# A recurrent block with six layers of local attention: the decays of a state in a PSUM bank, two small products more, and another order of the steps

## The chip, the cores and the metric

The kernel runs on one core of a Trainium2 chip. The time is the device time of one execution in microseconds. The kernel before took 3447.9 us, the median of three runs (3443.46 to 3448.29).

## The reference

The input x has 16 sequences of 256 rows of 128 numbers. After a layer norm two branches are computed from it, and their product is added to x.

```python
x = L0_attn_x
xn = _layernorm(x, axis=-1)
s = _L0_attn_ref(xn, ...)              # selective scan, 16 states per channel
g = _silu(_L0_ffn_ref(xn, ...))        # six layers of local attention and feed-forward
x = x + s * g
```

The first branch is a selective scan. With delta, u, B and C computed from xn by projections and short convolutions, each channel has 16 states, and state n decays with A = -(n + 1):

```python
dA = jnp.exp(d_t[..., None] * A)
h = dA * h + (d_t * u_t)[..., None] * B_t[:, None, :]
y = jnp.einsum('bdn,bn->bd', h, C_t)
```

The second branch has six layers. Each has 16 heads of width 64 with normed and rotated q and k, a softmax over a window of 32 rows and the 32 before them, an output product, and a gated feed-forward (gelu, inner width 341).

## The kernel before, in words

All work is laid out in iterations. A block is 128 rows of one sequence; a layer has 32 blocks and the six layers have 192. Iteration n does one step of each of many stages, for blocks at different distances: block n + 4 is projected to q and k, squared and rotated, block n + 2 is scaled and transposed, block n + 1 is scored, and block n is attended, divided and transposed. The list `order` (L759) says in which order the stages of one iteration are issued. The kernel is written with a manual schedule, so every engine takes its instructions in just that order, and waits at each until what it needs is there.

The attention runs so: `project` multiplies the rows with the q and k weights (L427), `values` with those of v. `square` (ACT, L438) and `lengths` (DVE, L504) make the sums of squares, `guess` (DVE) and `refine` (POOL) the inverse roots of two blocks at once, `rotate`, `rotate2` (DVE, L448 and L459) and `add` (POOL, L470) turn q and k, and `scale` (POOL, L542) multiplies with the inverse lengths. `turn` transposes q and k on PE (L552), and `turned_q` and `turned_k` copy them out of PSUM on ACT (L556). `score` writes a mask and then the products (L587, L601), `greatest` and `subtract` (DVE, L614 and L624) and `soften` (ACT, L633) make the weights, `turn_weights` and `turned_weights` transpose them, `attend` multiplies with the values (L657), and `divide_last` and `divide` (L673 to L681) divide. The last pair of heads (c = 7) has banks of its own, "e" and "l". `turn_out` and `turned_out` transpose the result, and after the second block of a sequence `close` multiplies with the output weights (L708): its first half ends an odd block's iteration, its second half belongs to the next iteration, as does `residual` (L718). `hand_out` copies v out of PSUM (L480) and lays it out with eight or ten DMAs on SP (L491 to L494).

The feed-forward of four blocks (a group of two sequences) is a generator of twelve pieces. `feed` takes the next piece and stands three times in `order`, so a group's feed-forward lasts four iterations: transposes and row statistics in the third piece, the norm in the fourth, transposes in the sixth, the first products in the ninth (L349, with gelu at L357), and the second in the eleventh (L372, with its residual at L375). In the last layer `end` (L388) follows when the last piece of a group is done: silu, the product with the first branch, four transposes on PE (L401), an add and a store.

The selective scan goes along with it: eight groups of 512 columns, one state per iteration. `clock` gives n from -2 to 17 for each group. `bring` loads the rows of B and C of state n + 2 to all partitions (SP), `decay` takes the exponential for the decays of state n + 1 (ACT, L296), `drive` multiplies B of state n + 1 with du (POOL, L301), `advance` scans state n (DVE, L288), `weigh` multiplies state n - 1 with C and adds it to y (POOL, L281 and L282), and `put_out` makes the output product. `before_scan`, taken a piece at a time by `prepare`, computes the next group's delta, du, B and C, with two convolutions on DVE (L220 and L227).

PSUM is one tile of eight banks of 512 numbers. The table `where` (L44) gives each use its bank; a name used by `pair` takes that bank and the next. A step that writes a bank waits until the earlier readers of that bank are done, so `where` and `order` together set the waits.

## Time and profile before

| | |
|---|---|
| runs | 3447.9 us median, 3443.46 to 3448.29 |
| the profiled execution | 3446.38 us, of which its span is 3444.6 us |
| PE busy | 3238.9 us (94%) |
| DVE busy | 2810.2 us (82%) |
| POOL busy | 2598.0 us (75%) |
| ACT busy | 2123.3 us (62%) |
| mean granted PE clock | 0.988 |
| scan, L288 | 128 times, 277.3 us, 2.17 us each |
| decays, L296 | 128 times, 80.6 us, 0.63 us each |

Busy time is the time in which an engine works at an instruction. PE is the matrix engine, PEld its loading of weights, DVE the vector engine, ACT the scalar engine, POOL the general one, and SP the one that issues most DMAs. In a group line the name before the arrow is what is written and the names behind it are what is read, with the number of instructions behind an x. What stands behind a vertical bar or in square brackets is idle time of the engine just before, and what ended it. In a line of a timeline the first number is the start and the second the length.

### The profile page before, as it was taken

Reading aid. Unit: us, or ns where it says so; the run is one execution under the profiler, and the core shown is the slowest. Engines: PE = TensorE matmul, PEld = TensorE weight load, DVE = VectorE, ACT = ScalarE, POOL = GpSimd, SP = SyncE. Lnnn points to the kernel's source line nnn. Section 1 sums busy time; section 2 is a strip of 40 time slices with the busy share of each in tenths; the row PEclk is TensorE's granted clock in tenths of the full one; section 3 lists DMA queues with packets and bytes.
Section 4 is the critical chain, followed back from the end, with each engine's and each line's share of the span. In section 5 each row is a group of like instructions: output and inputs, shape, how many; then the busy total and the mean of one; then the engine's idle time right before and its main releaser. Section 6 shows DMA issues by size and latency. Waiting matters only on the chain.

```text
span 3444.6 us, 139812 instructions
## 1 busy us (share of the span) xinstructions
PE 3238.9 (94%) x62080; PEld 2163.4 (63%) x62080; DVE 2810.2 (82%) x3705; ACT 2123.3 (62%) x2725; POOL 2598.0 (75%) x2358
## 2 busy tenths in 40 slices
PE   6999999999999999999999999999999999999986
PEld 3666666666666666666666666666666666666663
DVE  6898879887898789878987889788879987777663
ACT  4666657655666566656665666576666665666554
POOL 6688868986898589968996789688878996565550
PEclk9999999999999999999999999999999999999998
DMA  3433334433333334333333333334333432222222
GB/s 87 104 98 105 84 84 104 104 81 83 97 97 90 91 94 97 91 85 88 107 92 91 88 96 92 89 99 98 91 81 93 105 94 70 69 64 70 63 64 57
DMA packets 190680, 304.49 MB, mean 88 GB/s; under 512 B 32702, under 2 KB 56572, under 8 KB 190076
## 3 DMA queue, kind: packets, MB, share of 16 engines
q1 hardware_dynamic: 189788, 295.22, 33.9%
q8 instruction: 488, 8.00, 1.0%
q14 instruction: 116, 0.95, 0.1%
q10 hardware_dynamic: 288, 0.33, 0.0%
HBM read 94.81 MB, written 8.91 MB: 30 GB/s over the span
## 4 chain that ended last, share of the span: by engine, by line
PE 73%; DVE 12%; ACT 6%; POOL 5%; issue 4%; DMA 0%; SPq 0%; DVEq 0%; ACTq 0%; POOLq 0%
PE psum L427 23%; PE psum L552 14%; PE psum L708 9%; PE psum L657 7%; PE psum L349 7%; PE psum L601 6%; PE psum L372 3%; ACT oT L556 3%; DVE t L459 2%; DVE o L681 2%; PE psum L587 2%; DVE hs L288 1%; DVE t L448 1%; POOL t L470 1%; DVE cv L227 1%
## 5 line engine op out<-in xcount | busy, mean ns | idle before, releaser
L470 POOL TENSOR_TENSOR t<-t,t 128x1024 f32<-128x1024 f32 x384 | 957.1, 2502 | 355.0 <-DVE t L459 184.4
L427 PE MATMUL psum<-wqkv,xT 128*128 128x512 f32 x2304 | 1070.3, 600 | 18.6 <-DVE cv L227 7.2
L542 POOL TENSOR_TENSOR t<-t,y 128x1024 f32<-128x1024 f32 x384 | 723.1, 1905 | 7.5
L427 PEld LDWEIGHTS psum<-wqkv,xT 128*128 128x128 f32 x2304 | 417.4, 192 | 406.0 <-issue 304.5
L448 DVE TENSOR_TENSOR t<-psum,tab 128x1024 f32<-128x1024 f32 x384 | 467.9, 1219 | 143.9 <-PE psum L427 131.1
L556 ACT COPY aT<-psum 128x1024 f32<-128x1024 f32 x192 | 194.2, 1012 | 589.6 <-PE psum L552 589.6
L459 DVE TENSOR_TENSOR t<-psum,tab 128x1024 f32<-128x1024 f32 x384 | 465.9, 1213 | 0.0
L504 DVE TENSOR_REDUCE ss<-sq 128x16 f32<-128x1024 f32 x384 | 456.4, 1198 | 1.3
L552 PE MATMUL psum<-ident,t 128*128 128x128 f32 x3072 | 412.7, 277 | 20.8 <-POOL t L542 8.9
L438 ACT ACTIVATE sq<-psum 128x1024 f32<-128x1024 f32 x384 | 395.0, 1029 | 51.4 <-DVE t L459 51.0
L657 PEld LDWEIGHTS psum<-v,aT 64*32 64x32 f32 x24576 | 294.0, 105 | 200.9 <-issue 121.9
L708 PE MATMUL psum<-oT,wo 128*128 128x256 f32 x1536 | 357.5, 386 | 24.2 <-ACT oT L556 24.2
L657 PE MATMUL psum<-v,aT 64*32 64x65 f32 x24576 | 332.8, 227 | 47.0 <-issue 24.6
L552 PEld LDWEIGHTS psum<-ident,t 128*128 128x128 f32 x3072 | 340.4, 142 | 40.3 <-POOL t L542 11.7
L708 PEld LDWEIGHTS psum<-oT,wo 128*128 128x128 f32 x1536 | 283.8, 190 | 81.4 <-ACT oT L556 46.5
L480 ACT COPY vt<-psum 128x1024 f32<-128x1024 f32 x192 | 196.2, 1022 | 189.6 <-PE psum L427 189.6
L601 PEld LDWEIGHTS psum<-kT,qT 64*32 64x32 f32 x24576 | 282.8, 105 | 11.2 <-issue 0.8
L601 PE MATMUL psum<-kT,qT 64*32 64x64 f32 x24576 | 286.2, 226 | 0.0
L288 DVE TENSOR_TENSOR_SCAN hs<-dA,bc 128x512 f32<-128x512 f32 x128 | 277.3, 2166 | 0.0
L556 ACT COPY oT<-psum 128x1024 f32<-128x1024 f32 x192 | 194.8, 1014 | 124.9 <-PE psum L552 123.0
L349 PE MATMUL psum<-xn,w 128*128 128x512 f32 (+1 forms) x576 | 260.2, 601 | 6.0 <-ACT o L674 4.8
L624 DVE TENSOR_TENSOR at<-psum,top 128x1024 f32<-128x1024 f32 x192 | 235.1, 1225 | 25.3
(102 smaller groups left out, 4583.0 us busy)
## 6 DMA issues: line engine op xcount, KB each, us to landing
v<-vt SPq DMA_DIRECT2D x1152, 130.0 KB, 2.4
bc<-rows SPq DMA_DIRECT2D x128, 512.0 KB, 5.1
v<-vt SPq DMA_DIRECT2D x576, 65.0 KB, 2.5
wqkv<-in_Wqkv SPq DMA_DIRECT2D x18, 512.0 KB, 4.0
wo<-in_Wo SPq DMA_DIRECT2D x6, 512.0 KB, 4.0
first<-in_x SPq DMA_DIRECT2D x8, 256.0 KB, 5.0
xn<-xT SPq DMA_DIRECT2D x16, 128.0 KB, 2.4
pad<-xn SPq DMA_DIRECT2D x8, 256.0 KB
```

The costliest lines, as they stand in the source:

```text
L349: nc.tensor.matmul(ph[0:n, i * G : (i + 1) * G], w1[:, i * DI + c0 : i * DI + c0 + n], xn, start=True, stop=True,)
L427: nc.tensor.matmul(pq[:, cc], xb, wq[:, cc], start=True, stop=True)
L448: nc.vector.tensor_tensor(t1.rearrange("p (h d) -> p h d", h=H), b["pq", i].rearrange("p (h d) -> p h d", h=H), table(n, i, 0).unsqueeze(1 ...
L459: nc.vector.tensor_tensor(t2.rearrange("p (h f d) -> p h f d", h=H, f=2), b["pq", i].rearrange("p (h f d) -> p h f d", h=H, f=2)[:, :, ::- ...
L470: nc.gpsimd.tensor_tensor(b["qk", i], b["qk", i], b["t2", i], ALU.add)
L504: nc.vector.tensor_reduce(b["ss"][:, j * H : (j + 1) * H], b["sq", i].rearrange("p (h d) -> p h d", h=H), AX.X, ALU.add,)
L542: nc.gpsimd.tensor_tensor(t3, t3, b["inv"][:, j * H : (j + 1) * H].unsqueeze(2).to_broadcast([128, H, DH]), ALU.mult,)
L552: nc.tensor.transpose(pt[:, cc], of[:, cc], ident)
L556: nc.scalar.copy(to, pt.rearrange("p (c t) -> p c t", c=NP))
L601: nc.tensor.matmul(sc4[jj, r, c, :], qT[rr, c, jj], kT[rr, c, k0 : k0 + 64], start=False, stop=True, skip_group_check=True,)
L657: nc.tensor.matmul(b["pav7"][r][jj, 0:VW] if c == 7 else b["pav"][jj, r, c, :], aT[rr, c, jj], v2[rr, j, c * VW : (c + 1) * VW], start=Tru ...
L708: nc.tensor.matmul(b["pw"][:, 0:L], wo[:, c, :], b["oT"][:, c, :], start=(c == 0), stop=(c == NP - 1), skip_group_check=True,)
```

## The change

There are three parts. The decays of state n are written into PSUM bank 0 (name "d") in the same iteration in which they are scanned, in place of an SBUF tile one iteration ahead; bank 0 is also the first bank of k. In `attend`, two products of four columns come before the others, one for each half of the rows, into the banks of the last pair of heads, where the products of c = 7 then write over them. And `where` and `order` are others. In the new order the scan stands after the residual near the start of an iteration, v is projected right behind q, k is projected behind the transposes of the weights, k's transposes follow q's, and `soften` stands before two of the three `feed`.

```diff
-    where = dict(q="6", k="0", v="4", qT="4", kT="0", s="2", w="4", av="2", o="2", h0="6", h1="0", h2="4", e="7", l="6", pw="4", f="7", n="1")
+    where = dict(q="6", k="0", v="4", qT="2", kT="6", s="2", w="4", av="4", o="4", h0="2", h1="0", h2="4", e="3", l="2", pw="1", f="2", n="3", d="0")
...
     def decay():
         g, n = now
-        if 0 <= n + 1 < NS:
-            dA[n + 1] = mb.tile([128, G], FP, name="dA", bufs=2)
-            nc.scalar.activation(dA[n + 1], of[g]["delta"], AF.Exp, scale=-float(n + 2))
+        if 0 <= n < NS:
+            dA[n] = bank("d")
+            nc.scalar.activation(dA[n], of[g]["delta"], AF.Exp, scale=-float(n + 1))
...
         b["pav7"] = [bank("e"), bank("l")]
+
+        for r in range(2):
+            rr = slice(r * 64, (r + 1) * 64)
+            nc.tensor.matmul(
+                b["pav7"][r][0:W, 0:4], aT[rr, 7, 0:W], v2[rr, :, 0], start=True, stop=True
+            )
         for c in (7, 0, 1, 2, 3, 4, 5, 6):
```

The order of one iteration after the change, whole (that of before is at L759 to L807):

```python
    order = (
        (state, None, decay),
        (lengths, 3, 1),
        (norms_on, None),
        (guess, 3),
        (close, -1, 1),
        (residual, -1),
        (prepare, None),
        (project, 4, 0),
        (state, None, advance),
        (values, 1),
        (hand_out, 1),
        (feed, None),
        (score, 1),
        (refine, 3),
        (scale, 2, 0),
        (rotate, 4, 0),
        (greatest, 1),
        (turn_weights, 0),
        (project, 4, 1),
        (scale, 2, 1),
        (turned_weights, 0),
        (subtract, 1),
        (attend, 0),
        (state, None, weigh),
        (square, 4, 0),
        (divide_last, 0),
        (turn, 2, 0),
        (rotate2, 4, 0),
        (square, 4, 1),
        (turn, 2, 1),
        (turned_q, 2),
        (divide, 0),
        (turned_k, 2),
        (add, 4, 0),
        (rotate, 4, 1),
        (turn_out, 0),
        (rotate2, 4, 1),
        (lengths, 4, 0),
        (turned_out, 0),
        (state, None, bring),
        (soften, 1),
        (state, None, put_out),
        (feed, None),
        (state, None, drive),
        (add, 4, 1),
        (feed, None),
        (close, 0, 0),
    )
```

More of the change, by code (lines that the diff above doesn't have):

```diff
@@ L759, in tile_kernel @@
     order = (
+        (state, None, decay),
+        (lengths, 3, 1),
         (norms_on, None),
-        (lengths, 3, 1),
         (guess, 3),
@@ L764, in tile_kernel @@
         (residual, -1),
+        (prepare, None),
+        (project, 4, 0),
+        (state, None, advance),
+        (values, 1),
+        (hand_out, 1),
         (feed, None),
-        (project, 4, 0),
-        (prepare, None),
         (score, 1),
+        (refine, 3),
+        (scale, 2, 0),
         (rotate, 4, 0),
+        (greatest, 1),
         (turn_weights, 0),
-        (rotate2, 4, 0),
-        (greatest, 1),
-        (state, None, weigh),
-        (refine, 3),
-        (subtract, 1),
-        (scale, 2, 0),
-        (turned_weights, 0),
-        (project, 4, 1),
-        (square, 4, 0),
-        (state, None, bring),
-        (values, 1),
-        (scale, 2, 1),
+        (project, 4, 1),
+        (scale, 2, 1),
+        (turned_weights, 0),
+        (subtract, 1),
+        (attend, 0),
+        (state, None, weigh),
+        (square, 4, 0),
+        (divide_last, 0),
+        (turn, 2, 0),
+        (rotate2, 4, 0),
+        (square, 4, 1),
+        (turn, 2, 1),
+        (turned_q, 2),
+        (divide, 0),
+        (turned_k, 2),
         (add, 4, 0),
         (rotate, 4, 1),
-        (state, None, decay),
-        (hand_out, 1),
+        (turn_out, 0),
         (rotate2, 4, 1),
-        (add, 4, 1),
-        (attend, 0),
-        (divide_last, 0),
-        (state, None, drive),
-        (turn, 2, 0),
-        (divide, 0),
-        (state, None, advance),
-        (square, 4, 1),
-        (lengths, 4, 0),
-        (turned_q, 2),
-        (feed, None),
-        (feed, None),
-        (state, None, put_out),
-        (turn_out, 0),
-        (turned_out, 0),
-        (turn, 2, 1),
-        (turned_k, 2),
+        (lengths, 4, 0),
+        (turned_out, 0),
+        (state, None, bring),
+        (soften, 1),
+        (state, None, put_out),
+        (feed, None),
+        (state, None, drive),
+        (add, 4, 1),
+        (feed, None),
         (close, 0, 0),
-        (soften, 1),
     )
```

## The prediction

> **What bounds the kernel now.** I read the page's busy shares first, then the chain that ended last, then the queues in order of time.

> ```profile
> span 3444.6 us, 139812 instructions
> PE 3238.9 (94%) x62080; PEld 2163.4 (63%) x62080; DVE 2810.2 (82%) x3705; ACT 2123.3 (62%) x2725; POOL 2598.0 (75%) x2358
> PE 73%; DVE 12%; ACT 6%; POOL 5%; issue 4%; DMA 0%; SPq 0%; DVEq 0%; ACTq 0%; POOLq 0%
> ```

> TensorE (PE) sets the pace and nearly fills the span. So a gain on another engine counts only where PE waits for it. The busy times by stretch show how little that is in a stage that repeats (four iterations, 66.8 us) and in the last layer:

> ```profile
> 2600.00:2666.80 66.80, 65.72 (x1292) 44.36 (x1291) 60.84 (x77) 42.68 (x55) 60.94 (x53) 1.00 0.37 94
> 3000.00:3074.50 74.50, 68.22 (x1294) 45.75 (x1293) 51.90 (x73) 43.81 (x56) 40.89 (x41) 0.95 0.26 67
> ```

> The columns are the stretch, then PE, weight loads, DVE, ACT and POOL busy, the granted clock, and DMA. PE is busy 65.7 of 66.8 us, but the last layer takes 74.5 us for less work on DVE and POOL. The PE timeline gives the price of each step (start, length):

> ```profile
> 2601.40 0.41 PE L587 MATMUL psum<-mask,ident_h 64*32 64x512 bf16 x8
> 2603.07 1.09 PE L552 MATMUL psum<-ident,at 128*128 128x128 f32 x8
> 2604.00 3.60 PE L427 MATMUL psum<-wqkv,xT 128*128 128x512 f32 x8
> 2607.53 1.74 PE L657 MATMUL psum<-v,aT 64*32 64x65 f32 x128
> 2609.20 1.09 PE L552 MATMUL psum<-ident,t 128*128 128x128 f32 x8
> 2623.76 5.42 PE L349 MATMUL psum<-xn,w 128*128 128x512 f32 x12 [0.46 <-ACT o L674]
> 2631.16 3.72 PE L708 MATMUL psum<-oT,wo 128*128 128x256 f32 x16 [0.23 <-ACT oT L556]
> ```

> From start to next start: score 1.7, eight transposes 0.9, a projection 1.8, attend 1.7, half of close 1.7, first feed-forward products 5.2 (the second ones, at L372, 2.6). An iteration without feed-forward is then three projections 5.4, score 1.7, four transpose groups 3.5, attend 1.7, half a close 1.7: 14.0. Four of them with one feed-forward (5.2 + 2.6 + two transpose groups 0.9) come to 64.8, so some 2 of the 66.8 us are waits, in six or so places.

> **The change part by part.**

> *The scan.* Now a scan at L288 takes from 1.21 to 3.37 us (median 2.09), because it and POOL take turns:

> ```profile
> 2610.39 5.62 POOL L470 TENSOR_TENSOR t<-t,t 128x1024 f32<-128x1024 f32 x2
> 2610.68 3.16 DVE L288 TENSOR_TENSOR_SCAN hs<-dA,bc 128x512 f32<-128x512 f32 x1
> 2613.76 2.31 DVE L504 TENSOR_REDUCE ss<-sq 128x16 f32<-128x1024 f32 x2
> ```

> The scan starts inside POOL's first add (2.37 alone), ends 1.1 us after that one, and the second add takes 3.3. [...] DVE saves 277.3 − 128 × 1.21 = 122 us; POOL loses the long forms of L470 and L301, about 100 us. Neither is on PE's path: worth nothing by itself, and a margin below. The write at L296 is 0.63 us of ACT before; into PSUM I take the same. Its bank 0 is k's: the second projection now waits for the scan.

> *The order.* I follow one iteration through the queues, from PE's first q projection at 0, in iterations that end with a close ("odd"); the others ("even") begin with its second half, 1.7 us, and everything follows 1.7 later. PE: q and v to 3.6, score to 5.3, transposed weights and k to 8.0. Behind the last score the maximum starts 0.18 after the transposes do, subtract starts 1.35 later and takes 1.23: 8.05. Since e and l are now banks 3 and 2, the whole attend waits for that subtract: 8.1, where before it stood behind both k and v and only its later products touched those banks. Attend and the small products to 10.0, turned q to 10.85, turned k to 11.7, turned out to 12.6 (divide: 0.33 after attend, 0.28, 1.09, in time). ACT's copy of oT comes 1.1 after the start of its transposes and takes 1.0: 13.85; rotate2 of k, behind divide on DVE, ends at 13.8. Both hold back close (its bank 1 is k's), so PE waits 0.9 to 1.3 us where it waited 0.5. Close to 15.6.

> Even: the same chain puts attend at 9.8 and the end of turned out at 14.3; kT is copied behind qT on ACT until 14.7, and the next q, in banks 6 and 7, starts at 14.75.

> Feed-forward pieces fill these holes. Four iterations are: odd with small transposes 15.6; even with small transposes 14.75; odd with the 5.2 before close, where PE does not wait any more, 12.6 + 5.2 + 1.7 = 19.5; even with the 2.6 at the end 14.3 + 2.6 = 16.9. Together 66.8, against 66.8: the waits change place and the sum does not move. Taken as 0 ± 30 us over the 47 groups.

> Covers: k's wait for the scan is hidden in even iterations (residual ends at 3.0, scan at 4.2, k starts at 7.9). In odd ones DVE comes 1.7 us late with the lengths, starts the scan at 3.0 and ends the first rotate at 5.3, 0.2 before the maximum can start; what makes it later than that goes into attend one for one. decay stands behind soften on ACT and ends at 3.0 in the worst case, just in time. drive is issued on POOL late in the iteration before and ends 1.4 into this one. POOL, from the guess: refine 3.9, scales 3.8, weigh 2.6, add, drive 1.3, add, done 1.5 us before its next refine. On SP, hand_out's DMAs go out from 6.4 on, one iteration before attend reads them; bring now stands behind them and behind weigh (about 12.3), lands 5.1 us later, and drive reads it more than 10 us after that. Convolution (3.1 us of DVE, bank 3) now holds back score instead of k: about 2 us a group in odd iterations, where the waits for L227 now sum to 24 us over eight groups. first_norm uses the same bank, behind evictions long done.

> *The small products* do not exist in before. They are two of L657's kind on two of its eight tiles, each twice like every fp32 product here. Lower bound: two shares of 128 in 1.7 us, 0.03 us. Upper bound: they run alone (weights 0.105 and matmul 0.23 of those rows, twice) 0.4 us with the queue's extra waits (0.05 each) for the DMAs that they gather. I take 0.2, nearest to two sets of eight at the row's rate (0.1 each); 192 × 0.2 = 38 us, in the 66.8 above.

> *The last layer.* Each group ends with silu, product and transposes (L395 to L401), and PE has nothing else queued:

> ```profile
> 3059.37 1.53 DVE L375 SCALAR_TENSOR_TENSOR xT<-psum,b,xT 64x512 f32<-64x512 f32 x2 [1.08 <-PE psum L372]
> 3061.99 1.07 ACT L633 ACTIVATE at<-at 128x1024 f32<-128x1024 f32 x1
> 3063.07 1.28 ACT L395 ACT_TABLE_LOAD   x1
> 3064.37 1.28 ACT L395 ACTIVATE xn<-xT 64x512 f32<-64x512 f32 x2
> 3065.68 0.69 DVE L397 TENSOR_TENSOR xn<-xn,sT 128x512 f32<-128x512 f32 x1 [4.78 <-ACT xn L395]
> 3066.43 1.11 PE L401 MATMUL psum<-ident,xn 128*128 128x128 f32 x4 [5.42 <-DVE xn L397]
> ```

> xT is ready at 3060.9, but silu waits behind oT, kT, soften and a table load. In after, soften and the load come before xT is ready; the transposes of o and k (1.7 us), which stand behind L372 now, move ahead of it. From L372's end: 0.3, 1.5, last half of silu 0.6, product 0.7, in all some 3.4 us of idle PE instead of 5.4: 2.0 saved. [...] Six gaps × (2.0 + 1.4) = 20 us; with no change of clock 12.

> *Scattered waits.* The waits name DVE and POOL in some 100 places (us in total, times, longest):

> ```profile
> PEld psum L552 <- DVE o L681: 29.5, 76, 1.5
> PEld psum L657 <- DVE at L624: 17.9, 20, 1.2
> PEld psum L552 <- POOL t L542: 11.7, 13, 2.5
> ```

> About 60 us; part of it lies behind long scans and goes with them, part comes back in other places: 15, between 0 and 45.

> **Sum.** The profiled execution took 3446.4 us (its span and 1.8 around it; the median of the runs is 1.5 above): 3446 − 20 − 15 ± 0 = 3411.

> **Rivals.** (1) *Slower: DVE's 0.2 us in odd iterations is gone.* If the scan still takes 2.17 or waits for drive, attend comes 0.75 later in two of four iterations, in the 32 groups with scans: 48 us, so 3459; it outweighs the gains from a delay of 0.55 on (a scan of about 1.75 or more). [...] (2) *Same:* the small products cost 0.4, 38 more: 3449. The two-tile form runs alone, which speaks for it; that they overlap with what stands in the queue, against. (3) *Faster still:* small products at 0.05 and feed-forward pieces hiding most of close's wait, 0.8 and 0.3 per group less: 3411 − 29 − 14 = 3368. (4) *The scan is not faster and nobody cares:* only the last layer gains, 3426.

> **How the numbers follow.** Chances: my forecast 40%, (4) 8%, (3) 12%, (2) 10%, (1) and its like 30%. Measurements of this kernel tell no change from 0.2%, 7 us (the three runs lie within 5). Faster 40 + 8 + 12, less 3 for the forecast's own tail: 57%; same 11%; slower 32%. The likeliest case's own range is 3380 to 3440; for 8 in 10 I reach to (3) and past (1): 3365 to 3478.

> **What would show it.** L288 at 1.21 to 1.3 throughout and no L470 above 2.4: the scan step. Attend's first load released by L624, close by oT at about 1 us: the order. L655's two rows and the distance to the first L663: 0.2. Gaps of 3.4 before L401. I am wrong if maximum waits for DVE rather than for score, or if POOL's drive releases the scan.

## Result: slower by 3.4%, where 1.1% faster was forecast

The changed kernel takes 3561.4 us (median of 4 runs, 3556.8 to 3574.8), the kernel before 3448.1 us beside it. The ratio is 1.034, with a 95% interval of 1.032 to 1.036. Forecast were 3411 us and a range of 3365 to 3478: the sign was wrong, and the range did not hold the time.

The page of the changed kernel (span, busy shares, chain that ended last):

```profile
span 3555.0 us, 141696 instructions
PE 3290.0 (93%) x62848; PEld 2227.4 (63%) x62848; DVE 2699.4 (76%) x3705; ACT 2107.5 (59%) x2725; POOL 2488.4 (70%) x2358
PE 82%; ACT 5%; issue 5%; DVE 3%; DMA 3%; POOL 1%; SPq 0%; ACTq 0%; POOLq 0%; DVEq 0%
```

DVE and POOL lost about 110 us each, as forecast; PE is busy 51 us longer, and the span grew by 110. The groups of instructions show that the scan did what was expected of it, and what the small products (L655) are busy:

```profile
L470 POOL TENSOR_TENSOR t<-t,t 128x1024 f32<-128x1024 f32 x384 | 908.1, 2365 | 525.4 <-DVE t L459 264.0 <-PE psum L663 223.6 <-DVE den L686 29.2
L288 DVE TENSOR_TENSOR_SCAN hs<-psum,bc 128x512 f32<-128x512 f32 x128 | 156.5, 1223 | 21.1 <-issue 13.2 <-POOL less L170 3.9
L655 PE MATMUL psum<-v,aT 64*32 64x4 f32 x768 | 74.8, 168 | 26.2 <-ACT sq L438 7.8 <-ACT aT L556 6.2 <-issue 2.7
```

The waits of PE, with the us in total, how many, and the longest:

```profile
PE psum L663 <- issue: 64.6, 29, 5.2
PE psum L714 <- ACT oT L556: 38.6, 48, 1.3
PE psum L401 <- DVE xn L397: 36.1, 8, 5.4
PE psum L552 <- issue: 31.5, 31, 1.8
```

The first line has grown most. The same two rows before (attend was then at L657):

```profile
PE psum L657 <- issue: 24.6, 21, 3.0
PE psum L552 <- issue: 11.0, 15, 2.1
```

"Issue" means that the profile knows no wait: PE stands still in the middle of attend, or of the transposes behind it, with nothing to wait for. The busy times by stretch of a bad and of a good group of four iterations (columns as in the prediction) show what is at stake:

```profile
1191.00:1272.20 81.20, 71.20 (x1313) 47.97 (x1312) 60.79 (x83) 46.20 (x60) 47.43 (x45) 0.98 0.36 89
1344.60:1411.30 66.70, 65.73 (x1307) 44.99 (x1306) 55.93 (x76) 42.10 (x56) 55.13 (x53) 1.00 0.37 94
```

The good group takes 66.7 us, which is the number that the prediction had for the new order (66.8), but it is one of the shortest. Counted from an attend to the fourth one behind it, the 47 groups have a median of 71.4 us, against 68.7 before, and 34 of them are over 70 us, against 18 before. These make the loss. One stall in the timeline (start, length; in brackets the idle time before):

```profile
1015.73 1.88 PE L427 MATMUL psum<-wqkv,xT 128*128 128x512 f32 x4
...
1016.29 1.23 DVE L624 TENSOR_TENSOR at<-psum,top 128x1024 f32<-128x1024 f32 x1
...
1017.59 0.37 PEld L655 LDWEIGHTS psum<-v,aT 64*32 64x32 f32 x4 [0.81 <-ACT aT L556]
...
1017.88 1.56 PE L663 MATMUL psum<-v,aT 64*32 64x65 f32 x113
...
1022.06 0.34 PE L663 MATMUL psum<-v,aT 64*32 64x65 f32 x13 [2.61 <-issue]
```

The subtraction (L624) ends at 1017.52, attend's first weights are loaded at 1017.59, and after 1.9 us PE stops for 2.6 us with 13 products left. The stretch of the stall, and the one that begins 1.1 us behind it, show the second half of the price in the granted clock (third number from the end):

```profile
1019.40:1022.10 2.70, 0.09 (x10) 0.04 (x9) 0.26 (x1) 0.54 (x1) 2.29 (x1) 1.00 0.50 136
1023.20:1026.60 3.40, 3.40 (x19) 3.40 (x17) 3.40 (x4) 2.02 (x2) 0.43 (x2) 0.50 0.46 93
```

3.4 us at half clock follow, half of which is lost. In the middle of the run (from 70 us to the last layer's first output) there are 15 such windows, 54.6 us in all, and 14 of them stand directly behind a stall; before there were 3, 10.2 us.

The 110 us come from these parts, each the difference of the two traces: stalls put down to issue in the middle of the run, 36.6 to 94.1, +57; half clock over the whole run, 87.5 to 161.5 us, half of it lost, +37; waits that the profile names, in the middle of the run, 73 to 61, −12 (70 to 63 if only gaps over 0.15 us count); idle time in the last layer, +6; and 22 left over. The largest part of that rest is in attend: from its first instruction to the next stage it takes 1.94 us (median) where it took 1.63, 60 us over 192 iterations. The transposes of o, 1.19 to 0.87 us in the median, give part of it back.

### The profile page after: what moved, and what is told of

It is laid out like the page before. It is cut to its first block, busy times and chain, and to the rows that moved or that the text cites. A ratio compares the mean times of both kernels' runs of the same rounds, so it can differ in the third digit from the quotient of the medians.

```text
span 3555.0 us, 141696 instructions
## 1 busy us (share of the span) xinstructions
PE 3290.0 (93%) x62848; PEld 2227.4 (63%) x62848; DVE 2699.4 (76%) x3705; ACT 2107.5 (59%) x2725; POOL 2488.4 (70%) x2358
## 4 chain that ended last, share of the span: by engine, by line
PE 82%; ACT 5%; issue 5%; DVE 3%; DMA 3%; POOL 1%; SPq 0%; ACTq 0%; POOLq 0%; DVEq 0%
PE psum L427 24%; PE psum L552 18%; PE psum L714 9%; PE psum L663 8%; PE psum L349 7%; PE psum L601 7%; PE psum L372 3%; DMA v<-vt 2%; PE psum L587 2%; PE psum L655 2%; ACT oT L556 2%; ACT kT L556 1%; PE psum L181 1%; ACT L633 1%; DVE ss L504 1%
## 5 line engine op out<-in xcount | busy, mean ns | idle before, releaser
L470 POOL TENSOR_TENSOR t<-t,t 128x1024 f32<-128x1024 f32 x384 | 908.1, 2365 | 525.4 <-DVE t L459 264.0
L427 PE MATMUL psum<-wqkv,xT 128*128 128x512 f32 x2304 | 1074.2, 603 | 3.0 <-DVE t L459 1.5
L542 POOL TENSOR_TENSOR t<-t,y 128x1024 f32<-128x1024 f32 x384 | 723.0, 1904 | 7.6
L427 PEld LDWEIGHTS psum<-wqkv,xT 128*128 128x128 f32 x2304 | 425.5, 193 | 423.7 <-issue 393.5
L448 DVE TENSOR_TENSOR t<-psum,tab 128x1024 f32<-128x1024 f32 x384 | 464.8, 1210 | 44.0 <-PE psum L427 34.2
L459 DVE TENSOR_TENSOR t<-psum,tab 128x1024 f32<-128x1024 f32 x384 | 464.4, 1209 | 3.5 <-ACT sq L438 3.5
L504 DVE TENSOR_REDUCE ss<-sq 128x16 f32<-128x1024 f32 x384 | 458.7, 1206 | 1.3
L552 PE MATMUL psum<-ident,t 128*128 128x128 f32 x3072 | 407.9, 288 | 40.7 <-issue 26.1
L552 PEld LDWEIGHTS psum<-ident,t 128*128 128x128 f32 x3072 | 354.6, 147 | 69.4 <-issue 39.1
L663 PE MATMUL psum<-v,aT 64*32 64x65 f32 x24576 | 334.5, 226 | 64.7 <-issue 64.6
L614 DVE TENSOR_REDUCE top<-psum 128x16 f32<-128x1024 f32 x192 | 234.7, 1222 | 186.1 <-PE psum L601 186.0
L556 ACT COPY aT<-psum 128x1024 f32<-128x1024 f32 x192 | 194.3, 1012 | 260.0 <-PE psum L552 256.4
L663 PEld LDWEIGHTS psum<-v,aT 64*32 64x32 f32 x24576 | 290.8, 105 | 73.7 <-issue 66.7
L556 ACT COPY qT<-psum 128x1024 f32<-128x1024 f32 x192 | 195.0, 1015 | 229.3 <-PE psum L552 229.3
L349 PE MATMUL psum<-xn,w 128*128 128x512 f32 (+1 forms) x576 | 258.8, 599 | 0.9 <-ACT xn L338 0.9
L624 DVE TENSOR_TENSOR at<-psum,top 128x1024 f32<-128x1024 f32 x192 | 235.2, 1225 | 23.1 <-PE psum L552 3.2
```

What stands on the lines that cost most here:

```text
L349: nc.tensor.matmul(ph[0:n, i * G : (i + 1) * G], w1[:, i * DI + c0 : i * DI + c0 + n], xn, start=True, stop=True,)
L427: nc.tensor.matmul(pq[:, cc], xb, wq[:, cc], start=True, stop=True)
L448: nc.vector.tensor_tensor(t1.rearrange("p (h d) -> p h d", h=H), b["pq", i].rearrange("p (h d) -> p h d", h=H), table(n, i, 0).unsqueeze(1 ...
L459: nc.vector.tensor_tensor(t2.rearrange("p (h f d) -> p h f d", h=H, f=2), b["pq", i].rearrange("p (h f d) -> p h f d", h=H, f=2)[:, :, ::- ...
L470: nc.gpsimd.tensor_tensor(b["qk", i], b["qk", i], b["t2", i], ALU.add)
L504: nc.vector.tensor_reduce(b["ss"][:, j * H : (j + 1) * H], b["sq", i].rearrange("p (h d) -> p h d", h=H), AX.X, ALU.add,)
```

## Experiments

All times stand against runs of the kernel before on the same chip, whose median lay between 3446 and 3456 us from chip to chip, so kernels are compared by their ratios. A "stall" below is idle time of PE that is put down to issue, in the middle of the run.

### The small products

Run 1 leaves them out of the changed kernel, run 2 puts them alone into the kernel before.

```diff
-        for r in range(2):
-            rr = slice(r * 64, (r + 1) * 64)
-            nc.tensor.matmul(
-                b["pav7"][r][0:W, 0:4], aT[rr, 7, 0:W], v2[rr, :, 0], start=True, stop=True
-            )
```

> The changed kernel without its two small products ahead of attend; nothing else is altered. Theory A (the loss is TensorE's instruction fetch running dry inside attend and inside the transposes, because score and attend now stand 2.6 us apart; the small products add only their own time): the run of attend shortens from a median of 1.95 to 1.63 us, 192 x 0.32 = 61 us, so about 3500 us; the stalls put down to issue inside L663 (here at another line number) and L552 stay at 80 to 130 us. Rival B (the small products are the whole cost): 3450 us, and the stalls put down to issue fall to the 32 us that the kernel before has. Rival C (the small products only gather waits that attend would have anyway): 3550 us.

Measured: 3510.7 us, ratio 1.016 (1.014 to 1.019). The small products cost 1.8%, 62 us, in the changed kernel. Stalls stay at 81 us, 12 half-clock windows.

> The kernel before with the two small products alone put ahead of attend. Theory A: 192 x 0.25 to 0.32 us on TensorE's path, 3496 to 3509 us, and stalls put down to issue inside attend remain at about 24 us. Rival B (they are the whole cost): 3560 us. Rival C (they only gather waits): 3448 to 3455 us. The prediction's 0.2 us each: 3486 us.

Measured: 3471.6 us, ratio 1.005 (1.003 to 1.007): 17 us, 0.09 us an iteration. The same two products cost 0.32 us an iteration in one order and 0.09 in the other. They aren't the whole cost (rival B), and rival C is out too. Why they are dear in one place only comes out further down.

### The space between score and attend

At first I took the stalls for bursts: score and attend each issue some 260 instructions in 1.7 us, and in the new order stand 2.6 us apart instead of 4.4.

```diff
         (project, 4, 0),
+        (values, 1),
+        (hand_out, 1),
...
-        (values, 1),
...
-        (hand_out, 1),
```

> The kernel before with the value projection and its hand-out moved from behind the k projection to right behind the q projection, so that between the end of score and the start of attend only 2.7 us of TensorE work lies and no longer 4.5. Theory A (fetch): stalls put down to issue inside attend (L657) and the transposes (L552) rise from 32 us to 70 to 130 us, half-clock windows from 14 to 20 or more, and the time to 3490 to 3540 us. Rival D (the fetch is late because of the DMA traffic of hand_out and bring near attend, or the stalls belong to the small products): bring's transfers still lie where they lay and there are no small products, so the stalls stay at 20 to 40 us and the time at 3445 to 3460 us.

Measured: 3633.5 us, ratio 1.051. The run tells little: the moved v made new waits (184 of 0.5 us ahead of attend, put down to the squares), which I had not foreseen and which are half of the 178 us. Stalls stayed at 38 us, against the 70 to 130 expected.

Run 4 gives the changed kernel the space back.

```diff
-        (project, 4, 0),
...
         (values, 1),
...
         (score, 1),
...
-        (rotate, 4, 0),
...
         (turn_weights, 0),
+        (project, 4, 0),
...
         (subtract, 1),
+        (rotate, 4, 0),
...
-where = dict(... v="4", ...)
+where = dict(... v="6", ...)
```

> The changed kernel with the q projection (and its first rotate, behind subtract) moved from ahead of score to behind the transposed weights, and the bank of v set from 4 to 6 so that no new wait arises: between the end of score and the start of attend lie 4.4 us of TensorE work again, as in the kernel before. The small products stay. Theory A (fetch): stalls put down to issue inside attend and the transposes fall from about 130 us to 30 to 50, half-clock windows from 30 to about 18, and the time to 3561 - 80 - 35 = about 3450 to 3480 us. Rival B (small products) and rival D (DMA traffic): stalls stay above 100 us and the time at 3545 to 3570 us.

Measured: 3511.3 us, ratio 1.016 (1.015 to 1.018), 61 us taken back, with the small products in. The waits of PE:

```profile
PE psum L663 <- issue: 37.4, 36, 2.0
PE psum L587 <- DVE cv L227: 32.5, 14, 3.6
PE psum L587 <- ACT xn L338: 25.0, 38, 1.2
PE psum L552 <- issue: 7.9, 9, 1.5
```

Stalls halve (94 to 51 us) and none is longer than 2.0 us. Two new waits of score for its banks (convolution, feed-forward) eat a part of the gain, and 8 of the 9 half-clock windows that are left stand behind gaps of this kind, none behind a stall. Taking them away:

```diff
-where = dict(... n="3", ...)
+where = dict(... n="5", ...)
...
-        (soften, 1),
         (state, None, put_out),
         (feed, None),
         (state, None, drive),
         (add, 4, 1),
         (feed, None),
+        (soften, 1),
         (close, 0, 0),
```

> The kernel of the run before with q behind the transposed weights, with two of its new waits taken away: the convolution's bank n set from 3 to 5, so that score no longer waits for the convolution, and soften moved behind the two later feed-forward steps on ScalarE, so that score no longer waits for the copy at L338. Small products stay. Theory A: waits of score fall by 45 us and the half-clock windows that follow them (11 in the middle of the run) by most, so 3511 - 45 - 20 = about 3440 to 3455 us. If half-clock windows do not follow from these waits: 3465 us. If the waits only move to the transposed weights: 3500 us.

Measured: 3460.6 us, ratio 1.002 (1.001 to 1.003). Three windows of half clock, no wait of score above 10 us in sum. The same without the small products:

> The same without the two small products. Theory A: in this order stalls in attend are short, so they cost what they cost in the kernel before (16 us) rather than the 50 us that they cost in the changed kernel: about 3425 to 3440 us, which would be faster than the kernel before. Rival B (the small products cost 50 us wherever they stand): 3390 to 3405 us.

Measured: 3454.5 us, ratio 1.000 (0.998 to 1.001). Here the small products cost 0.2%, 8 us. So all but 0.2% of the loss can be undone by where q and soften stand and by the banks of v and of the convolution; the expected gain on top of it did not come.

That the bursts as such are the cause falls with the next run, which takes half of score's products away:

```diff
-        for c in range(NP):
+        for c in range(0, NP, 2):
```

> The changed kernel with score computing only every second pair of heads (c = 0, 2, 4, 6; the other four pairs of heads keep the mask values and their scores are left out): 128 fewer TensorE instructions and about 0.7 us less TensorE work in each iteration; the distance from the end of score to attend stays 2.6 us, the DMA traffic stays the same. Theory A (two bursts of some 260 instructions each, too close for the fetch of 256 at a time): stalls put down to issue inside attend and the transposes fall from 95 to under 40 us, half-clock windows from 30 to under 20; 3561 - 134 - 57 - 25 = about 3345 us. Rival D (late fetch through DMA traffic, or stalls that belong to attend and its operands): stalls stay at 80 us or more and the time at about 3427 us.

Measured: 3452.4 us, ratio 0.999; score takes 0.44 us less (1.62 to 1.18 in the median), which is 84 us of the 122. Stalls stay at 88 us, 18 windows. Theory A in its first form is wrong: with 128 instructions fewer per iteration the stalls did not go.

### DMA traffic

The stalls coincide with packets of the queue that brings instructions. Among the DMA queues on the page of the changed kernel it has 496 packets (the columns are packets, MB and a share of time), 16 KB each; its 125,696 TensorE instructions make 253 a packet, and with the 1,403 semaphore instructions of the same queue 256:

```profile
q8 instruction: 496, 8.13, 1.0%
```

Of the 34 stalls of 1.5 us or more in the changed kernel, PE goes on again 1.4 us (median) after such a packet has landed. The packet starts as late as 0.5 us (median) before PE runs dry. And hand_out's DMAs now run from 2 us before attend to 5 us after its start, where before they began 2 us behind it. So traffic was the next suspect. The next run leaves hand_out's DMAs out from block 8 on, counted from 0 (attend then multiplies with the values of earlier blocks).

```diff
-        for r in range(2):
+        for r in range(2) if n < 8 else ():
```

> The changed kernel without hand_out's eight or ten DMAs from the eighth block on (the copy of v on ScalarE stays; attend then reads the values of the first blocks, so this part of the computation is left out). Every TensorE instruction stays. In the changed kernel these DMAs run from 2 us before attend begins to 5 us after it (130 to 180 KB in each us), in the kernel before they begin 2 us after attend has begun. Theory D (their traffic delays the packets that bring TensorE's instructions, and attend and the transposes run dry behind it): stalls put down to issue fall from 94 us (last layer aside) to 20 to 40, half-clock windows there from 16 to 2 to 5, time 3561 - 60 - 25 = 3465 to 3485 us. Theory A (dense instruction bursts alone): stalls stay at 80 us or more and the time at 3545 to 3565 us.

Measured: 3553.1 us, ratio 1.029 (1.028 to 1.031). PE's waits of this run:

```profile
PE psum L663 <- issue: 81.7, 32, 5.7
PE psum L552 <- issue: 46.5, 35, 3.1
```

More stalls, not fewer, and of 47 of 1.5 us or more in the whole run, 24 have almost nothing else in flight (under ten packets). Those end after 2.2 us at most; all above 2.6 us have 84 packets or more beside them, here bring's. Traffic makes a stall longer but doesn't make it. The next three runs say the same from the other side. They issue hand_out's DMAs behind bring:

```diff
+    def send(n):
...
         (state, None, bring),
+        (send, 1),
```

> The changed kernel with hand_out split in two: the copy stays where it is, the DMAs are issued behind bring on SP (which itself waits for weigh), some 5 us later, so that they fall behind attend and the transposes. Nothing is left out. Theory D: stalls put down to issue fall to 40 to 60 us, half-clock windows to 3 to 8, time 3475 to 3505 us. Theory A: 3545 to 3565 us. If the copy of the next v comes to wait for these DMAs: above 3565 us.

Measured: 3641.7 us, ratio 1.056. Without the small products:

> The same without the two small products. Theory D, with the small products at 16 us as in the kernel before: 3460 to 3490 us; with the small products at 50 us: 3425 to 3455 us. Theory A: 3495 to 3515 us.

Measured: 3562.8 us, ratio 1.032, against 1.016 with the DMAs early. On the version with q moved and no small products:

> The version with q behind the transposed weights, its two banks and soften moved, and no small products (3454.5 us), with the DMAs of hand_out issued behind bring as well. Theory D: its 55 us of stalls put down to issue fall to about 30, so 3425 to 3440 us, faster than the kernel before by 0.4 to 0.9%. Theory A: 3450 to 3460 us.

Measured: 3481.9 us, ratio 1.009, against 1.000. In each pair the stalls of 1.5 us or more got longer (means of 3.0, 2.8 and 2.5 us, against 2.2, 2.0 and 2.0).

### The scan, put back into SBUF

```diff
-            dA[n] = bank("d")
+            dA[n] = mb.tile([128, G], FP, name="dA", bufs=2)
```

> The changed kernel with the decays written into an SBUF tile (two buffers) in place of PSUM bank 0; step, order, banks and small products stay. Theory A (the loss is fetch stalls, half clock and small products, not the scan): the scan at L288 rises from 1.22 us to a mean of about 2 and long forms of L470 come back, but the time stays within 1% of 3561 us. The prediction's rival 1 (DVE has 0.2 us of margin in odd iterations, a scan of 1.75 or more goes into attend): +48 us, about 3610. If instead the second projection's new wait for the scan (bank 0) costs something, the time falls below 3540.

Measured: 3668.7 us, ratio 1.063 (1.061 to 1.065): 99 us more than the changed kernel. That is the prediction's first rival, at twice its price. The group of the scan in this run:

```profile
L288 DVE TENSOR_TENSOR_SCAN hs<-dA,bc 128x512 f32<-128x512 f32 x128 | 233.1, 1821 | 28.0 <-issue 14.4 <-POOL bc L301 7.1 <-POOL t L470 4.4
```

One of its iterations in the timeline:

```profile
2640.02 3.38 DVE L288 TENSOR_TENSOR_SCAN hs<-dA,bc 128x512 f32<-128x512 f32 x1 [0.25 <-POOL bc L301]
...
2645.74 1.23 DVE L624 TENSOR_TENSOR at<-psum,top 128x1024 f32<-128x1024 f32 x1
...
2647.07 0.40 PE L655 MATMUL psum<-v,aT 64*32 64x4 f32 x3 [2.35 <-issue]
```

A scan of 3.38 us ends at 2643.4; rotate, maximum and subtraction come later by as much; the subtraction ends at 2646.97 and attend's first weights load at 2647.04. The profile says "issue" before L655, 68 us in 33 waits, because the wait is not on the product itself but on a semaphore instruction ahead of it in PE's queue. This line gave the theory that held: in the changed kernel, too, attend starts 0.07 us behind the subtraction, in 158 of the 164 iterations of the middle.

### Theory S: the head of attend is held

The trace also has the semaphore instructions of PE's queue. Attend has five in each iteration of the changed kernel (with the small products, which gather its DMA waits), one and a half before. From the view of line L655 of the changed kernel (duration shortest, median, longest in ns):

```profile
L655 PEldq EVENT_SEMAPHORE  x960: 51/51/3347, 73.9 to 3502.6; - x192
```

From where these are executed I took how far PE's queue has been read ahead. In the kernel before it is 2.2 us (median) ahead of attend's first product; in the changed kernel 0.05 us behind it. What stands behind such a wait waited with it: in the changed kernel the third of the five waits, from 2.64 to 0.06 us before attend's first product (medians of 191 iterations), and the two behind it are executed after it. Before, none of these instructions took longer than 0.05 us:

```profile
L657 PEldq EVENT_SEMAPHORE  x286: 51/51/51, 71.3 to 3396.7; - x143
```

Theory S is that the packet with the next 256 instructions is then asked for only when attend is already running through its 264.

Three runs were to take the hold away with PE's order kept. The first computes heads 7 last (without small products), the second halves the maximum, the third leaves it out.

```diff
-        for c in (7, 0, 1, 2, 3, 4, 5, 6):
+        for c in (0, 1, 2, 3, 4, 5, 6, 7):
```

> The changed kernel without the small products and with attend's pair of heads 7 computed last in place of first, so that only attend's last 64 of 256 instructions write banks 3 and 2 and wait for the subtraction; its head then waits for nothing later than the copy of aT, 0.6 us before it starts. To be compared with the changed kernel without the small products (3510.7 us; attend begins 0.07 us after the subtraction's end in nearly all of its iterations, and 16% of them have a stall of over 1.3 us put down to issue). Theory S (TensorE's queue is read ahead only up to a wait that isn't met; held at attend's head until the moment attend begins, it asks for its next 256 instructions too late, and attend runs dry 1.7 us later): stalls outside the last layer fall from 81 to 35 to 60 us, half-clock windows there from 13 to about 6, time 3460 to 3485 us. Rival A (dense bursts alone) or D (DMA traffic): 3505 to 3515 us.

Measured: 3588.0 us, ratio 1.042. I had overlooked a wait; PE's waits name it:

```profile
PE psum L552 <- ACT o L675: 178.8, 178, 1.2
```

The q transposes share bank 2 with heads 7 and now wait 1.0 us in each iteration for their copy. Stalls inside attend fell from 46 to 21 us, but these pauses give the packets time as well, so the run proves nothing.

```diff
-            top.rearrange("p r c -> p (r c)"),
-            pscore.rearrange("p (h k) -> p h k", h=H),
+            top[:, 0, :],
+            pscore[:, 0:512].rearrange("p (h k) -> p h k", h=NP),
```

> The changed kernel with the maximum taken over the first half of the heads alone (the other half of the maxima is left out, and subtract uses those of the first half for both), which makes the maximum about 0.6 us shorter and the subtraction's end about 0.55 us earlier; TensorE's instructions, their order and the DMAs stay. Theory S: attend is held until about 0.6 us before it starts (by aT's copy and the subtraction); stalls fall from 94 us to 55 to 80, time 3510 to 3545 us. Rivals A and D: 3550 to 3565 us.

Measured: 3500.1 us, ratio 1.017 (1.015 to 1.019).

```diff
-        nc.vector.tensor_reduce(
-            top.rearrange("p r c -> p (r c)"),
...
+        b["top"] = zero
```

> The changed kernel without the maximum (zeros are subtracted in its place, so this part of the computation is left out): the subtraction ends about 1.2 us earlier, the head of attend is then held only by the copy of aT, 0.6 us before it starts; TensorE's instructions, their order and the DMAs stay. Theory S: stalls fall from 94 us to 50 to 75, time 3500 to 3535 us, close to the run with half a maximum, since aT's copy holds then. Rivals A and D: 3550 to 3565 us.

Measured: 3494.9 us, ratio 1.015 (1.013 to 1.017). Both are some 60 us faster than the changed kernel, while the stalls stay at 89 and 92 us. The semaphore instructions are now executed 0.16 and 0.19 us ahead of attend, since aT's copy holds its head too: enough that reading the five of them no longer lies in attend (1.69 and 1.74 us instead of 1.94, 0.2 × 192 = 38 to 48 us, most of the gain), not enough for the packet. So the theory's forecast for the stalls was wrong here, by the amount of the read-ahead that these edits could free.

The last two runs set the hold apart from the order. The first starts from the best version (q, banks and soften moved, no small products), with oT copied in two halves:

```diff
-        evict(b["oT"][:, :, t0 : t0 + 128], b["pt", 3])
+        for c in range(0, NP, 4 if b["blk"] else NP):
+            cs = slice(c, c + (4 if b["blk"] else NP))
+            nc.scalar.copy(b["oT"][:, cs, t0 : t0 + 128], ...)
```

> The version with q behind the transposed weights, its two banks, soften moved and no small products (3454.5 us), with the copy of oT on ScalarE made in two halves for the second block of a pair, so that close's first four products wait for the first half alone. Its 47 waits of 0.8 us for oT shrink to about 0.3: 3454 - 47 x 0.5 = 3431 us, within 3425 to 3445, faster than the kernel before by 0.3 to 0.9%. If these waits are hidden elsewhere: 3450 to 3460 us.

Measured: 3441.5 us, ratio 0.999 (0.998 to 1.000), which can't be told from the kernel before. Close's waits did not shrink by much: it waits 49 times, 0.76 us each where it was 0.82, and 31 of the 49 now end with rotate2 on DVE (L459) and not with the copy. What this run has over the same version without the split is 17 us less in stalls. Then, in this version, the subtraction is moved behind one rotate on DVE, and not one TensorE instruction changes place:

```diff
-        (subtract, 1),
         (rotate, 4, 0),
+        (subtract, 1),
```

> The best version so far (3441.5 us: q behind the transposed weights, two banks and soften moved, no small products, copy of oT in halves) with the subtraction on VectorE moved behind the first rotate of q, nothing else. The subtraction then ends about 0.6 us before attend starts instead of 1.8 us before, still early enough that attend needn't start later. Theory S: attend's semaphore instructions, now read 1.5 us (median) before attend starts, are read 0 to 0.4 us before it; stalls put down to issue rise from 38 us to 70 to 100 us, half-clock windows (last layer aside) from 3 to 8 to 16, time 3480 to 3515 us. If read-ahead plays no part and the order of TensorE's work alone decides: stalls 35 to 55 us and 3435 to 3455 us.

Measured: 3723.2 us, ratio 1.080 (1.078 to 1.082). From the timeline:

```profile
2496.32 1.22 DVE L624 TENSOR_TENSOR at<-psum,top 128x1024 f32<-128x1024 f32 x1
2497.63 1.68 PE L658 MATMUL psum<-v,aT 64*32 64x65 f32 x121 [0.85 <-ACT sq L438]
...
2502.27 0.44 PE L658 MATMUL psum<-v,aT 64*32 64x65 f32 x7 [2.95 <-issue]
```

The rotate waits for q, so the subtraction ends later than I had worked out and attend waits 0.8 us for it in 188 iterations, 155 us (the profile names the squares, but what ended last, 0.09 us before, is L624). Only 125 of the 280 us would be left for other things, and they are what theory S says: stalls 38 to 118 us, half-clock windows 3 to 32, 143 us of half clock where there were 14.

The second starts from the changed kernel without the small products. It moves v ahead of q and the transposed weights ahead of score, and computes heads 7 fourth, so that nothing holds attend's head, while score and attend stand closer than ever:

```diff
-        (project, 4, 0),
...
         (values, 1),
         (hand_out, 1),
+        (project, 4, 0),
...
+        (turn_weights, 0),
+        (turned_weights, 0),
         (score, 1),
...
-        (turn_weights, 0),
...
-        (turned_weights, 0),
...
-        for c in (7, 0, 1, 2, 3, 4, 5, 6):
+        for c in (0, 1, 2, 7, 3, 4, 5, 6):
```

> The changed kernel without the small products, with the transposed weights moved from behind score to ahead of it (v first, then q, transposed weights, score, k, attend) and the pair of heads 7 computed fourth in attend: its head then waits neither for the copy of aT (made 3 us earlier) nor for the subtraction, while score and attend stand even closer (1.9 us instead of 2.6). A new wait comes with it: v, now first, waits for oT's copy in every second iteration, some 0.8 us x 96 = 77 us. Theory S: semaphore instructions of attend are read 1 us or more before it, stalls put down to issue fall from 81 to 30 to 60 us. Dense bursts or the order alone: stalls stay at 80 to 120 us. Time 3510 + 77 - 60 = about 3530 us by theory S, 3590 us or more otherwise.

Measured: 3586.1 us, ratio 1.040. PE's waits:

```profile
PE psum L658 <- DVE at L624: 21.5, 94, 2.1
PE psum L658 <- issue: 19.6, 49, 1.4
PE psum L552 <- issue: 18.7, 23, 2.6
```

The time is no better than the theory's rival gave, because the edit brought more waits of its own than I had counted: attend takes 2.15 us, since heads 7 wait for the subtraction in its middle. The stalls are as theory S has them: their sum is 43 us, against 81 in the same kernel with its head held, and it is made of short pieces. The long ones are gone: 2 of 1.5 us or more, against 32, and 2 half-clock windows against 12.

All kernels together; "ahead" is the median time by which attend's semaphore instructions are executed before its first product, "packets" the number of instruction packets that start between 1.0 us before this product and 0.75 us behind it, of 488 or so (400 with half of score):

```
kernel                              ahead us  packets  stalls >= 1.5 us  half-clock windows  ratio
before                                 2.20        38          7                  3           1.000
small products alone                   1.91        48         12                  5           1.005
q between                              1.57        61          6                  9           1.016
 + banks, soften                       1.57        55          9                  3           1.002
 ... without small products            1.46        55         11                  4           1.000
 ... and DMAs late                     1.51        47         12                 10           1.009
 ... oT in halves (DMAs early)         1.46        56          5                  3           0.999
weights ahead of score                 2.10        43          2                  2           1.040
heads 7 last                           0.55        14         10                  9           1.042
no maximum                             0.19         4         31                 12           1.015
half a maximum                         0.16         0         33                 13           1.017
no DMAs of hand_out                    0.08         0         42                 23           1.029
half of score                          0.04         1         30                 18           0.999
v early in the kernel before           0.00         3         15                 19           1.051
changed kernel                        -0.05         0         31                 15           1.034
 without small products               -0.05         1         32                 12           1.016
 DMAs late                            -0.05         1         44                 33           1.056
 DMAs late, no small products         -0.05         2         31                 21           1.032
held again (best version)             -0.05         0         37                 32           1.080
scan in SBUF                          -0.11         0         56                 35           1.063
```

(Of the 56 in the last row up to 31, those ahead of attend, are waits for the subtraction.) With 0.5 us or more ahead there are 2 to 12 long stalls, with less 30 to 56, in any order of TensorE's work, with and without small products and DMAs. One row doesn't fit: v early, with 15. Its attend waits 0.5 us for the squares each time; why it stalls less than the others is open.

When a packet is asked for isn't recorded, but its start is, and the starts follow the hold. The changed kernel's wait ends 0.06 us before attend's first product; no packet starts from 1.0 us before this product to 0.75 us behind it, and 172 of the 496 start from 1.0 to 2.5 us behind it. In "held again" the wait lasts from 5.27 to 0.06 us before the product, and 2 of 488 packets start from 4.0 us before it to 1.0 us behind it. The best version has such a wait too, but from 4.33 to 1.72 us before: there 4 packets start from 3.0 to 1.0 us before the product, and 56 in the stretch that the column counts. In all three the starts stop some 1.2 us after the wait begins and come back some 1.2 us after it is over. Which instruction of the 256 gives the request stays open.

## Why the prediction was wrong, step by step

*What bounds the kernel.* Right: PE sets the pace, 93% busy. Read too narrowly: only PE's named waits and its work were counted. PE's supply of instructions was not asked about, though the row of L657 and issue stood at 24.6 us, second in the list of PE's waits.

*The scan.* Right in size: all 128 scans take 1.21 to 1.23 us, L470 is at 2365 ns, and DVE and POOL lost 111 and 110 us (122 and 100 forecast). The 1.21 us was the shortest scan of before, and the time of L448, which reads one operand from PSUM and one from SBUF: 172 of its 384 instructions have POOL at work for 95% or more of their time, and take 1.21 to 1.23 us like the others (the kernel before; shortest, median and longest in ns):

```profile
L448 DVE TENSOR_TENSOR t<-psum,tab x384: 1206/1215/1226, 15.9 to 3330.3; 128x1024 f32<-128x1024 f32 x192
```

The changed kernel's trace agrees: with the decays in PSUM no scan is above 1.23 us, where the longest took 3.37. That a read from PSUM takes the scan longer can't be seen (mean 1223 ns; the shortest scan takes 1.21 us before and after). "Worth nothing by itself" is right only against the kernel before: within the new order, in SBUF, the longer scan (mean 1.82 us) costs 99 us more (the run with the scan put back), because the rest of the order has no slack left for it.

*The order: this is the step that failed.* "Behind the last score the maximum starts ...: 8.05. Since e and l are now banks 3 and 2, the whole attend waits for that subtract: 8.1." The times are right to 0.1 us (from the start of q to attend the median is 8.1), and a group without stalls comes near the 66.8. The step failed where it read a margin of 0.05 us as free. In fact attend starts 0.07 us after the subtraction nearly always, where the median distance before was 1.05; the wait in PE's queue ends only then, 0.06 us before attend's first product. Of the 57 + 37 us of stalls and half clock, the runs with the head held and free show that most go with it (stalls 81 to 43 us, half-clock windows 12 to 2 when it is freed); its reading of semaphores makes attend 0.3 us longer on top. I had written 0 ± 30 us for it.

*Close and its wait for oT* was to be 0.9 to 1.3 us; it is 0.8 in 47 of them. Right, a little too dear.

*The small products.* 0.2 us an iteration forecast; 0.09 us in the kernel before, 0.04 in the version with q moved, 0.32 in the changed kernel. The bounds (0.03 to 0.4) held, though the terms listed for the upper one, 0.105 and 0.23 twice, come to 0.67; and rival 3 names 0.8 us a group where its 29 us rest on 4 × 0.15 = 0.6. The price went with where the semaphores that they gather are executed: 1.91 and 1.57 us ahead of attend where it is 0.09 and 0.04, 0.05 us behind its start where it is 0.32.

*The last layer, −20 us:* wrong, it became 16 us longer (461 to 477 us from 8 us before the first output on). The 20 counts 1.4 us a gap for a shorter time at half clock, a term that no run shows: with each of the first six of the eight gaps before L401 (4.2 to 5.4 us) the changed kernel has 6.83 us at a granted clock of 0.50, and the kernel before (5.4 to 6.6 us) 6.83 five times and 3.41 once. The gap before L401 stayed at 5.3 us, as the timeline of the changed kernel shows:

```profile
3079.00 1.28 ACT L633 ACT_TABLE_LOAD   x1
...
3080.30 1.06 ACT L633 ACTIVATE at<-at 128x1024 f32<-128x1024 f32 x1
...
3081.37 1.28 ACT L395 ACT_TABLE_LOAD   x1
...
3082.67 1.28 ACT L395 ACTIVATE xn<-xT 64x512 f32<-64x512 f32 x2
3083.98 1.72 DVE L397 TENSOR_TENSOR xn<-xn,sT 128x512 f32<-128x512 f32 x1 [1.90 <-ACT xn L395]
...
3085.75 1.11 PE L401 MATMUL psum<-ident,xn 128*128 128x128 f32 x4 [5.31 <-DVE xn L397]
```

I had soften done before xT is ready. It has a table load of its own here, 1.28 us, which the earlier place (behind close) did not have in that iteration, so silu's load waits until 3081.4. And L397, two SBUF inputs beside POOL's scale at L542, takes 1.72 us where it took 0.69 (1.7 to 1.8 us in four of the eight groups). With soften behind the feed-forward steps (the version with banks and soften moved) that load is gone and the gap is near the 3.4 that I had forecast; its timeline:

```profile
3005.00 1.08 ACT L633 ACTIVATE at<-at 128x1024 f32<-128x1024 f32 x1
...
3006.10 1.28 ACT L395 ACT_TABLE_LOAD   x1
...
3010.12 1.12 PE L401 MATMUL psum<-ident,xn 128*128 128x128 f32 x4 [3.49 <-DVE xn L397]
```

*Scattered waits, −15:* right. Named waits in the middle fell from 73 to 61 us.

*Rivals.* The slower one named the place, attend behind the subtraction, but asked for DVE to be later than planned by 0.55 us before it decides. It needed nothing: on time was already too late. The sign of being wrong that it named, a maximum that waits for DVE, would not have shown it; L614 waits for score, 186 us, just as planned.

## What to carry to other kernels

A semaphore wait at the head of a dense run of TensorE instructions cost more here than the idle time that the plan showed for it: in the changed kernel a wait that ended just in time, 0.06 us before attend, came with no packet start from 1.0 us before attend to 0.75 us into it, and with 31 long stalls. A wait as long did little harm where it ended early: in the best version it ends 1.7 us before attend, and there are 5 long stalls. So plan for more than a microsecond between the last operand of such a run and its start (1.4 us or more ahead gave 2 to 12 long stalls here), and put long matmuls with few instructions in between, as q's projection was here (four products in 1.9 us), not only as cover for the operand. When TensorE stands still for "issue" in the middle of a run, look at the semaphore instructions ahead of it and at the instruction packets among the DMAs, and count the half-clock windows behind the stalls in the price (15 in the middle of the changed kernel, 54.6 us, half of it lost).
